# VectorE's instructions kept in source order through the middle of a four-layer transformer kernel, with the split queries' rest written in place

## The chip, the cores and the metric

The kernel runs on one core of one Trainium2 chip. The time is the device time of one execution in microseconds (us); of several executions the median is given. A profiled execution of the same program gives the trace. The engines are TensorE (PE: matrix products and transposes; PEld its weight loads), VectorE (DVE), ScalarE (ACT), GpSimd (POOL) and SyncE (SP, which issues the DMAs here). Each engine runs its own list of instructions, and semaphores make one engine wait for another.

## The reference

Four layers run one after the other over x, four batches of 512 tokens by 512 channels, each added to x with a gate. Cut to what matters:

```python
def _wkv(w, u, k, v):                 # a scan over the tokens, for each channel
    def step(carry, kv_t):
        p, q, o = carry
        no = jnp.maximum(o, u + kt); A = jnp.exp(o - no); E = jnp.exp(u + kt - no)
        y = (A * p + E * vt) / (A * q + E)
        no2 = jnp.maximum(w + o, kt); A2 = jnp.exp(w + o - no2); E2 = jnp.exp(kt - no2)
        return ((A2 * p + E2 * vt, A2 * q + E2, no2), y)

def _L0_ffn_ref(x, w1, w2, w3):       # 512 -> 2048 -> 512
    # _bitlinear(x, w): x in int8 steps by groups of 64, w by its sign and mean magnitude
    h = jax.nn.silu(_bitlinear(x, w1)) * _bitlinear(x, w2)
    return _bitlinear(h, w3)

def _L1_xattn_ref(x, cond, wq, bq, wkv, bkv, wp, bp):    # 16 heads of 32
    q = _qdq(x) @ _qdq(wq).T + bq                        # _qdq: int8 steps, a scale for each row
    k, v = jnp.split(cond @ wkv.T + bkv, 2, axis=-1)
    attn = jax.nn.softmax(jnp.einsum('bnhd,bmhd->bhnm', q, k) * scale, axis=-1)
    o = jnp.einsum('bhnm,bmhd->bnhd', attn, v).reshape(B, N, C)
    return _qdq(o) @ _qdq(wp).T + bp

def _L1_ffn_ref(x, gamma, W):         # rms norm, int8 steps, W in {-1, 0, 1}
    return jnp.einsum('bsd,od->bso', x_ste, w_ste)

x = x + tanh(g_xattn[0]) * _L0_xattn_ref(..., _layernorm(x), ctx)    # WKV
x = x + tanh(g_ffn[0]) * _L0_ffn_ref(_layernorm(x), ...)             # FFN
x = x + tanh(g_xattn[1]) * _L1_xattn_ref(_layernorm(x), ctx, ...)    # attention
x = x + tanh(g_ffn[1]) * _L1_ffn_ref(_layernorm(x), ...)             # ternary
```

## The kernel before, in words

**Merged streams.** Each layer of each batch is a Python generator that emits some instructions and yields. `line(gen, parts)` gives a generator places, a number for each of its steps, on one axis; `run(until)` always advances the generator with the lowest place, and so several layers of different batches are merged into one stream of emitted instructions. The unit of the axis is a batch, cut in `SLOTS` = 17 slots, one for each of the 16 units of an FFN and one more. In the steady part the FFN of batch b runs in the slots from b on, beside the WKV layer of batch b+1 and the attention of batch b−1, which begins some five slots later. The ternary layer of a batch comes after its attention's output projection. `run(0.99)` emits the first part, with the weights' preparation under way, inside a block with its own pools; after it the attention's pool is opened, and `run(NB + 9)` emits all that remains. There are NB = 4 batches; the last attention runs from place 4.29 on.

**The order on the engines.** The order of emission is not the order of execution. A list scheduler sorts the instructions of each engine by its own estimates of when their inputs are ready. TensorE is bound to the source: `matmul()` and `transpose()` go through `in_turn`, and `next_turn()` moves on the instruction behind which those of the next step must stand (L162, L165 are these helpers, so every matmul and transpose has one of these two lines). VectorE, ScalarE, POOL and SP have no such bond. A block `tc.manual_schedule(engines={...})` takes the order of emission for the engines named.

**An FFN unit** is a block of 128 tokens (t) by 512 hidden channels (f). Two products of eight matmuls each go to ff_hp. ScalarE takes the tanh (L745), VectorE makes the gate (L746) and the product with the second half (L750). `quantised` then brings the result to int8 steps: the maximum by groups (L222, tile qg_s), its scale (L676, L678), the product rounded to int8 (L680) on VectorE, a cast on ScalarE (L684), and a product on POOL (L685). `parts` transposes the result (tp_ps), and writes it as a rounded half (ScalarE, L696) and the rest (VectorE, L697). The down product goes to ff_acc, which L773 adds to x.

**The WKV layer** of batches 1 to 3 is four chains of 128 channels, eight steps apart. In each VectorE has the scans L599, L629 and L634, the product L632, the reciprocals L640 (two halves), the product L645 and the addition L653; POOL has L608, L628, L630, L635, L636, L641 and L642.

**The attention.** `prepared` (L219 POOL, then at_s by L222, L226, L227 on VectorE, L231 ScalarE, transposes qr_ps) brings the rows of x to int8 steps. `project(g)` makes the queries of 128 channels: VectorE's L898 into q, ScalarE's L903 with the rounded half, VectorE's L904 with the rest, and two DMAs on SP to qD, from where the units' queries are fetched again (at_qR). Its tiles q and half, as at_xn, tf_xn and at_y, are rows of one pool tag, at_row, with `ROWS` = 3 buffers. A unit is a pair of heads by 256 tokens: scores s_ps, their maximum (VectorE, L948, one number for each row), the exponentials with their sum (ScalarE, L950), transposes pt_ps, copies (ScalarE, L970), the product with the values o_ps (L990 copies it), and `collect` (ot_ps; L998 and L1000 on VectorE). `project_out` makes the scale at_s of the output rows (L222, L226, L227), rounds (L231), and after the product VectorE's L1036 and an addition (L1037).

**The ternary layer** centres and scales a row on POOL (L219, L1147, tile tf_xn), takes its maximum and scale on VectorE (tile tf_s: L222, L1151, L1152, L1158, L1159), rounds on ScalarE (L231), transposes (qr_ps), multiplies (f_ps), adds (L1172) and writes the output.

**PSUM** has eight banks. After the first part, three (hp) are shared by ff_hp and s_ps, three (m) by most transposes and small products, and two are ff_acc.

Of the kernel before, what the change touches and what calls it, by code (L numbers as in the profile page):

```python
# [11 lines left out]
F32R = mybir.dt.float32r  # L12
# [18 lines left out]
def kernel(  # L31
# [37 lines left out]
    NB, T, D = x.shape  # L69
# [61 lines left out]
    def bank(name, dtype=F32):  # L131

        return psum_tile(name, "m", dtype)
# [22 lines left out]
    def next_turn():  # L156

        if "last" in turn:
            turn["ahead"] = turn["last"]

    def matmul(*args, **kwargs):
        return in_turn(nc.tensor.matmul(*args, **kwargs))  # L162
# [677 lines left out]
    def attention_layer(b, xb, pool, tiles=range(NT)):  # L840
# [5 lines left out]
        lo, n = tiles[0] * P, len(tiles) * P  # L846
# [9 lines left out]
        def row(name, dtype=F32):  # L856
            return pool.tile([P, D], dtype, name=name, tag="at_row", bufs=ROWS)
# [29 lines left out]
        def project(g):  # L887
            qp = bank("q_ps")[:, 0:n]
            for c in range(NC):
                matmul(  # L890
                    qp,
                    lhsT=wqT[:, c, g * P : (g + 1) * P],
                    rhs=xqT[:, c, lo : lo + n],
                    start=(c == 0),
                    stop=(c == NC - 1),
                )
            q = row("at_q")[:, 0:n]
            nc.vector.scalar_tensor_tensor(  # L898
                q, qp, sq[:, g : g + 1], sxb[:, lo : lo + n], ALU.mult, ALU.mult
            )  # L900
            half = [row("at_half", F32R)[:, 0:n] for _ in range(2)]
            bias = bqc[:, g : g + 1]
            nc.scalar.activation(half[0], q, AF.Identity, bias=bias)  # L903
            nc.vector.scalar_tensor_tensor(  # L904
                half[1], q, bias, half[0].bitcast(F32), ALU.add, ALU.subtract
            )
            for i in range(2):
                nc.sync.dma_start(out=qD[b][g][i, :, lo : lo + n], in_=half[i].bitcast(F32))
# [83 lines left out]
        def collect(k):  # L992
# [14 lines left out]
            )  # L1007

        project(0)
        fetch_keys(0)  # L1010
        fetch_values(0)
        fetch_queries(0)
        yield
        project(1)
        fetch_queries(1)
        yield
# [45 lines left out]
        for k in range(len(units) + 2):  # L1062
# [29 lines left out]
            if now:  # L1092
                p, h = units[k]
                if h == 0:
                    if p + 1 < NP:
                        fetch_keys(p + 1)
                    if p % 2 == 0 and p // 2 + 2 < NC:
                        next_turn()
                        project(p // 2 + 2)
                elif p % 2 and p // 2 + 1 < NC:  # L1100
                    fetch_values(p // 2 + 1)
                if k + 2 < len(units):
                    fetch_queries(k + 2)
# [72 lines left out]
    def ternary_layer(b, xb, pool):  # L1176
        if b == NB - 2:
            r, scale = statistics(b, xb, range(NT))
            yield
        else:  # L1180
            r, scale = layernorm(xb, rms=True, pinned=False), None
        yield from in_steps([ternary(b, xb, pool, t, r, scale) for t in range(NT)], 1)
# [9 lines left out]
    def late(make):  # L1192
        yield from make()

    def place(line):

        k = line["step"]
        for start, end, steps in line["parts"]:
            if k < steps:
                at = start + (end - start) * k / steps  # L1200

                return (math.floor(at * SLOTS) + 0.8) / SLOTS if line["aside"] else at
            k -= steps
        return end

    def run(until):
        while lines:
            now = min(lines, key=place)
            if place(now) > until:
                return  # L1210
            try:
                next(now["gen"])
                now["step"] += 1
                next_turn()
            except StopIteration:
                lines.remove(now)
# [5 lines left out]
    def line(gen, *parts, aside=False):  # L1222
        lines.append({"gen": gen, "parts": parts, "step": 0, "aside": aside})
# [124 lines left out]
    for b in range(NB):  # L1348
        if b:
            early = (0.99, 1.0, 4) if b == 1 else (b - 0.19, b - 0.1, 3), (b - 0.08, b, 1)  # L1350
            line(
                late(lambda b=b: ffn_layer(xs[b])),
                *((early[0],) if b == 1 else early),
                (b, b + 16 / SLOTS, 64),
                (b + 16 / SLOTS, b + 17.75 / SLOTS, 7),
            )
        start = b + 1 + 4.95 / SLOTS
        end = start + 18 / SLOTS
        line(
            late(lambda b=b: attention_layer(b, xs[b], at)),  # L1360
            (b + 1.0 if b == 0 else b + 0.7, b + 1.03 if b == 0 else b + 0.9, 5),
            (b + 1 + 1.7 / SLOTS, b + 1 + 3.7 / SLOTS, 5),
            (b + 1 + 3.75 / SLOTS, b + 1 + 4.35 / SLOTS, 2),
            (start, end, 72),
            (end, end + 2.4 / SLOTS, 6)
            if b != NB - 2
            else (end - 0.15 / SLOTS, end + 4.65 / SLOTS, 6),
            (end + 2.4 / SLOTS, end + 3.4 / SLOTS, 4),
        )
        if b < NB - 1:  # L1370
            line(
                late(lambda b=b: ternary_layer(b, xs[b], at)),
                (end + 3 / SLOTS, end + 8 / SLOTS, 8)
                if b < NB - 2
                else (end + 4.85 / SLOTS, end + 11.85 / SLOTS, 7),
                aside=b < NB - 2,
            )
    run(NB + 9)


# [43 lines left out]
```

## Time and profile before

| | |
|---|---|
| median of 3 runs | 1096.12 us (1095.92 to 1096.5) |
| the profiled execution | 1094.21 us |
| its span, first to last instruction | 1092.4 us |
| its mean granted TensorE clock | 0.956 |
| PE busy | 943.3 us (86% of the span) |
| VectorE busy | 827.0 us (76%), 1600 instructions |
| ScalarE busy | 729.9 us (67%) |
| POOL busy | 320.7 us (29%) |
| DMA | 189.68 MB, mean 174 GB/s |
| 0 to 316 us (first part) | PE busy 262.98, VectorE 214.17 |
| 316 to 330 us | PE busy 9.42, VectorE 11.57 |
| 330 to 1092.4 us | PE busy 670.87, VectorE 601.26 |

A line of a timeline or a group reads: start and duration in us (or busy time and mean), engine, source line, operation, the tile written and after the arrow the tiles read, shape and type, and "xN" where N like instructions are drawn together. A bracket at its end gives the idle time of that engine just before and, after the arrow, the instruction on another engine that ended it.

The page also draws the span in 40 equal slices of 27.3 us; a digit is the busy share in tenths:

```profile
PE   3879997998879888799997886999999999878975
DVE  5985548757876899896769898966687866579976
PEclk8889999999999999999999798999999999989998
```

After the first part PE's row dips twice, in the 14th to 17th slice (355 to 464 us: 8 8 8 7) and in the 22nd to 25th (573 to 683 us: 7 8 8 6); VectorE's row is at 8 to 9 there.

### The profile page before, as it was taken

To read this page: it belongs to the slowest core of one execution; us is meant where nothing else is said; L and a number is where in the kernel's file an instruction comes from. 1 tells how busy PE (TensorE), PEld (TensorE's weight loads), DVE (VectorE), ACT (ScalarE), POOL (GpSimd) and SP (SyncE) were. 2 spreads that over 40 slices of the span, in tenths; PEclk is the share of its full clock that TensorE was granted. 3 is DMA by queue.
4 is the path that set the end of the run, shared out by engine and by line. 5 is a ranking of instruction groups with operands and counts; after the bars stand their busy time and mean duration, and the time that the engine had idled before them with its cause. 6 is when DMAs were issued, how large, how long until landed. Compare 5 with 4: busy or idle time off the path is not lost.

```text
span 1092.4 us, 17928 instructions
## 1 busy us (share of the span) xinstructions
PE 943.3 (86%) x6350; PEld 680.0 (62%) x6380; DVE 827.0 (76%) x1600; ACT 729.9 (67%) x1490; POOL 320.7 (29%) x328
## 2 busy tenths in 40 slices
PE   3879997998879888799997886999999999878975
PEld 2345564565557666677775665677776777655652
DVE  5985548757876899896769898966687866579976
ACT  5656755567545776667877576677685777877863
POOL 3831104423333254621215545412122410100000
PEclk8889999999999999999999798999999999989998
DMA  8188845464445674645576354655574563244311
GB/s 288 39 272 317 323 169 190 144 221 155 154 146 181 221 234 127 231 129 169 185 234 204 121 177 133 204 195 180 184 231 156 184 210 116 59 148 116 116 42 39
DMA packets 85674, 189.68 MB, mean 174 GB/s; under 512 B 12241, under 2 KB 36817, under 8 KB 74577
## 3 DMA queue, kind: packets, MB, share of 16 engines
q1 hardware_dynamic: 85584, 188.53, 51.7%
q8 instruction: 51, 0.84, 0.3%
q14 instruction: 39, 0.31, 0.1%
HBM read 148.65 MB, written 39.85 MB: 173 GB/s over the span
## 4 chain that ended last, share of the span: by engine, by line
PE 49%; DVE 22%; ACT 14%; POOL 5%; issue 5%; DMA 4%; SPq 1%; ACTq 0%; POOLq 0%; DVEq 0%
PE ff_hp L162 15%; PE pt_ps L165 7%; PE ff_acc L162 6%; PE o_ps L162 4%; PE v_ps L162 4%; PE s_ps L162 3%; ACT at_P L950 3%; DVE wk_q L640 3%; ACT at_PT L970 3%; DVE at_nm L948 2%; PE k_ps L162 2%; DVE wk_p L634 1%; PE qr_ps L165 1%; PE tp_ps L165 1%; ACT wk_e L612 1%
## 5 line engine op out<-in xcount | busy, mean ns | idle before, releaser
L162 PE MATMUL ff_hp<-wT,xp 128*128 128x512 f32 x1024 | 275.7, 412 | 6.6 <-DVE ff_z L746 3.7
L162 PEld LDWEIGHTS ff_hp<-wT,xp 128*128 128x128 f32 x1024 | 195.4, 196 | 54.6 <-DVE ff_z L746 5.7
L950 ACT ACTIVATE at_P<-s_ps,at_nm 128x512 f32<-128x512 f32 x256 | 175.0, 690 | 45.2 <-DVE at_nm L948 43.4
L948 DVE TENSOR_REDUCE at_nm<-s_ps 128x1 f32<-128x512 f32 x256 | 166.6, 677 | 38.4 <-PE s_ps L162 37.9
L970 ACT COPY at_PT<-pt_ps 128x512 f32<-128x512 f32 x224 | 131.2, 590 | 72.6 <-PE pt_ps L165 71.9
L685 POOL TENSOR_TENSOR ff_z<-qg_b,qg_s 128x512 f32<-128x512 bf16 x64 | 71.9, 1124 | 314.6 <-ACT qg_b L684 304.7
L165 PE MATMUL pt_ps<-ident,at_P 128*128 128x128 f32 x1024 | 155.4, 280 | 9.0 <-ACT at_PT L970 4.3
L165 PEld LDWEIGHTS pt_ps<-ident,at_P 128*128 128x128 f32 x1024 | 118.1, 142 | 47.3 <-ACT at_PT L970 10.9
L162 PE MATMUL ff_acc<-wT,hr 128*128 128x512 f32 x512 | 137.6, 409 | 5.2 <-DVE hr L697 2.6
L162 PE MATMUL s_ps<-at_kR,at_qR 128*128 128x512 f32 x256 | 103.0, 464 | 24.0 <-ACT at_P L950 17.6
L162 PEld LDWEIGHTS ff_acc<-wT,hr 128*128 128x128 f32 x512 | 92.9, 191 | 26.2 <-DVE hr L697 4.2
L162 PE MATMUL o_ps<-at_PT,at_V 128*32 128x128 f32 x2048 | 75.4, 281 | 4.7 <-ACT at_PT L970 2.8
L162 PEld LDWEIGHTS o_ps<-at_PT,at_V 128*32 128x32 f32 x2048 | 54.8, 111 | 28.6 <-issue 11.6
L746 DVE SCALAR_TENSOR_TENSOR ff_z<-ff_z,ff_hp 128x512 f32<-128x512 f32 x64 | 43.4, 679 | 37.0 <-ACT ff_z L745 36.9
L745 ACT ACTIVATE ff_z<-ff_hp,coef 128x512 f32<-128x512 f32 x64 | 44.1, 688 | 40.5 <-PE ff_hp L162 38.1
L750 DVE SCALAR_TENSOR_TENSOR ff_z<-ff_hp,coef,ff_z 128x512 f32<-128x512 f32 x64 | 47.7, 745 | 30.2 <-PE ff_hp L162 30.1
L684 ACT CAST qg_b<-qg_i 128x512 bf16<-128x512 int8 x80 | 49.3, 617 | 27.4 <-DVE qg_i L680 17.3
L162 PEld LDWEIGHTS s_ps<-at_kR,at_qR 128*128 128x128 f32 x256 | 43.3, 194 | 36.4 <-ACT at_P L950 25.2
L162 PE MATMUL v_ps<-wkvT,cT 128*128 128x512 f32 x128 | 60.5, 618 | 5.5 <-DVE wT L303 2.3
L162 PE MATMUL k_ps<-cT,wkvT 128*128 128x512 f32 x128 | 61.3, 631 | 2.3 <-ACT wk_k L584 1.0
L640 DVE RECIPROCAL wk_q<-wk_q 128x256 f32<-128x256 f32 x32 | 54.5, 1722 | 3.0 <-POOL wk_q L635 1.6
L696 ACT CAST hr<-tp_ps 128x512 fp32r<-128x512 f32 x64 | 37.6, 588 | 21.7 <-PE tp_ps L165 21.7
(180 smaller groups left out, 1669.4 us busy)
## 6 DMA issues: line engine op xcount, KB each, us to landing
wT<-wD SPq DMA_DIRECT2D x72, 1024.0 KB, 5.4
wn<-in_L_ffn_w_dram SPq DMA_DIRECT2D x18, 1024.0 KB, 6.2
at_kR<-kD SPq DMA_DIRECT2D x128, 128.0 KB, 4.0
at_qR<-qD SPq DMA_DIRECT2D x256, 64.0 KB, 2.5
wD<-wT SPq DMA_DIRECT2D x12, 1024.0 KB, 4.2
kD<-k_half SPq DMA_DIRECT2D x16, 512.0 KB, 2.8
qD<-at_half SPq DMA_DIRECT2D x32, 256.0 KB, 2.2
cn<-in_ctx_dram SPq DMA_DIRECT2D x8, 512.0 KB, 5.9
```

What stands on the lines that cost most here:

```text
L162: return in_turn(nc.tensor.matmul(*args, **kwargs))
L165: return in_turn(nc.tensor.transpose(*args))
L640: nc.vector.reciprocal(half, half)
L684: nc.scalar.copy(qb, qi)
L685: nc.gpsimd.tensor_tensor(grouped(src), grouped(qb), s.unsqueeze(2).to_broadcast([P, NG, GS]), ALU.mult)
L696: nc.scalar.copy(part[:, 0, :], pt)
L745: nc.scalar.activation(z, hp, AF.Tanh, scale=coef[:, 0:1])
L746: nc.vector.scalar_tensor_tensor(z, z, 1.0, hp, ALU.add, ALU.mult)
L750: nc.vector.scalar_tensor_tensor(z, hp, coef[:, 1:2], z, ALU.mult, ALU.mult)
L948: nc.vector.tensor_reduce(nm, sp, AX.X, ALU.max, negate=True)
L950: nc.scalar.activation(lanes[k, i, t], sp, AF.Exp, bias=nm, accum_out=sums[k][:, t, i : i + 1],)
L970: made[k] = nc.scalar.copy(dst, blocks(pt))
```

## The change

Two edits. In `project` the rest of the queries is no longer a row of its own: it is written over q, which is its input. And between the end of the first part and place NB + 0.4 = 4.4, everything is emitted inside a block in which VectorE takes the order of emission; from 4.4 on, the order is the scheduler's again, as it is before place 0.99.

```diff
-            half = [row("at_half", F32R)[:, 0:n] for _ in range(2)]
+            half = [row("at_half", F32R)[:, 0:n], q.bitcast(F32R)]
             bias = bqc[:, g : g + 1]
             nc.scalar.activation(half[0], q, AF.Identity, bias=bias)
             nc.vector.scalar_tensor_tensor(
@@
+    with tc.manual_schedule(engines={mybir.EngineType.DVE}):
+        run(NB + 0.4)
     run(NB + 9)
```

## The prediction

> **What bounds the kernel now.** I read three views: the table by stage, the timeline of TensorE at its longest stall, and VectorE's timeline around that stall and in a quiet unit.
>
> The table by stage cuts the profiled execution where the work beside the FFN changes: microseconds, then the busy time of each engine with its instructions, then TensorE's granted clock.
>
> ```profile
> 370.00:470.00 100.00, 84.43 (x574) 64.86 (x575) 94.57 (x148) 69.48 (x145) 50.76 (x50) 0.95 0.57 186
> 470.00:570.00 100.00, 96.01 (x786) 75.74 (x788) 73.82 (x172) 76.03 (x168) 20.76 (x22) 1.00 0.56 185
> 570.00:692.00 122.00, 96.88 (x643) 73.11 (x641) 108.78 (x193) 81.88 (x163) 64.61 (x62) 0.90 0.52 168
> 692.00:790.00 98.00, 95.14 (x760) 74.37 (x761) 69.36 (x159) 71.35 (x158) 20.80 (x21) 1.00 0.58 193
> ```
>
> Columns two and four are TensorE and VectorE. From 470 to 570 and from 692 to 790 TensorE is busy 96 and 97% and sets the pace. In the two stretches that carry the WKV of batch 2 (370 to 470, "stretch 1") and batch 3 (570 to 692, "stretch 2"), TensorE falls to 84 and 79%, and VectorE is the fullest engine: 95 and 89%. VectorE idles 5.4 us in stretch 1 and 13.2 us in stretch 2. Only in these two, and in the 14 us between the first part and 330, can VectorE's order gain time; in the rest it can only lose some.
>
> Why stretch 2 idles more shows on TensorE's timeline (start, duration, last in brackets the idle time before and what ended it):
>
> ```profile
> 651.85 0.60 PE L165 MATMUL tp_ps<-ident,ff_z 128*128 128x128 f32 x4
> 661.05 1.11 PE L165 MATMUL qr_ps<-ident,tf_xn 128*128 128x128 f32 x4 [8.60 <-ACT tf_xn L231]
> ```
>
> The ternary layer's transposes wait 8.6 us for a row that ScalarE rounds at 660.18, and ScalarE waits for a scale from VectorE. That scale is five small operations, and VectorE's timeline shows where they stand:
>
> ```profile
> 639.79 0.69 DVE L222 TENSOR_REDUCE tf_s<-tf_xn 128x1 f32<-128x512 f32 x1 [0.40 <-POOL tf_xn L1147]
> ...
> 657.07 0.10 DVE L1151 TENSOR_SCALAR tf_s<-tf_s 128x1 f32<-128x1 f32 x1
> ...
> 658.80 0.15 DVE L1152 RECIPROCAL tf_s<-tf_s 128x1 f32<-128x1 f32 x1
> 658.88 1.15 DVE L1159 TENSOR_TENSOR tf_s<-tf_s,coef 128x1 f32<-128x1 f32 x1
> ...
> 660.03 0.12 DVE L1158 TENSOR_SCALAR tf_s<-tf_s 128x1 f32<-128x1 f32 x1
> ```
>
> Between the maximum at 639.79 and the next link lie 17 us of other work that the scheduler put first. The output projection's scale is torn in the same way (L222 594.70, L226 596.13, L227 597.92) and TensorE stands 3.87 us before 599.47; 2.70 us more stand ahead of 615.65, where transposes wait for L1036. Together 15.2 us of TensorE stall in stretch 2, and after each the matmuls are slow for a while: eight ff_hp at 663.67 take 3.32 us, against 2.01 elsewhere.
>
> **The change, part by part.** It adds and removes no instruction. VectorE takes its work in the order in which the code emits it from the end of the first part (about 316 us) to place 4.4, the first two units of the last attention (about 950 us). The other engines keep the scheduler's orders; those move in places, as the built kernels show: POOL's L608 and L598 now stand behind L685, and single pt_ps transposes change sides with s_ps.
>
> In an FFN unit the source emits L222, L676, L678, L680 as one run; the scheduler interleaves other work. A run of dependent links is slower:
>
> ```profile
> 336.56 0.69 DVE L222 TENSOR_REDUCE qg_s<-ff_z 128x8 f32<-128x512 f32 x1
> 337.28 0.17 DVE L676 TENSOR_SCALAR qg_s<-qg_s 128x8 f32<-128x8 f32 x1
> 337.48 0.20 DVE L678 RECIPROCAL qg_r<-qg_s 128x8 f32<-128x8 f32 x1
> 337.72 0.69 DVE L680 TENSOR_TENSOR qg_i<-ff_z,qg_r 128x512 int8<-128x512 f32 x1
> ```
>
> From start to start, medians over the trace: L750 to L222 785 ns (668 with something else next), L222 to L676 702 (600), L676 to L678 205 (70), L678 to L680 237 (118). That is 1.93 against 1.45 us: 0.48 lost for each unit. Stretch 1 and 2 hold some 8 units each, so +3.8 us each.
>
> The projections of the queries (L898, ScalarE's L903, L904) become adjacent on VectorE: L904 waits there for ScalarE, with everything behind it. Three adjacent pairs in this trace run 1.59, 1.59 and 1.95 us from start to start, against 0.67 when not held, so the wait is 0.9 to 1.3; I take 1.1. Two projections for each stretch: +2.2 each. Behind L904 stands L697 of the same unit, which the down projection wants. The Trainium skill, page "PSUM — Partial Sum Buffer", section "Engine vs sequencer instructions", calls VectorE's queue strictly first in, first out; the interleaved case avoids that hold, so the rule speaks against the change, and priced by the three rows it is this same +2.2.
>
> The in-place edit is free in instructions. It takes two rows of the three-buffer pool for a projection instead of three. In this trace L904 of the projection at 641.8 stood until 662.3, after the stalled transposes of tf_xn had given their row back. In strict source order L904 stands ahead of the very chain that would free that row, so I read the edit as what makes the order possible, and cost it at 0. Its cover: the second write to qD must read q before that row is reused, and a qD write lands 2.2 us after issue, while the next projection comes a unit (10 us) later. Without this cover it costs 2.2 us each.
>
> Two-input operations on VectorE take longer beside POOL. L632 lasts 1.33 us on average; where it follows L629 directly, it takes 0.69 and POOL's L630 the delay (1.72 against 1.28):
>
> ```profile
> 610.23 0.69 DVE L632 TENSOR_TENSOR wk_q<-wk_e,wk_q 128x512 f32<-128x512 f32 x1
> ```
>
> The source always has L629, L632 adjacent, so L632's excess leaves: 2.6 us in stretch 1 and 1.6 in stretch 2. The Trainium skill, "SBUF — State Buffer", section "Who interferes with whom", makes this an exclusive lock on a shared port pair; by it the loser waits out the whole other operation (1.28 us for L630), where the rows show about 0.7 lost, and the sum by it would be some 2 us a stretch better. L904's excess (1.0 beside L630 in stretch 1) leaves too, as L904 stands elsewhere, and the excess of L1159 and L198 (2.9 in stretch 2), since the tf_s chain closes up. I can't exclude that other pairs collide anew: the excess over all lines is 7.1 and 9.1 us, so the bounds of this term are −3.6 to +3.6 in stretch 1, −4.5 to +4.5 in stretch 2.
>
> The torn chains close. In source order the at_s and tf_s chains are consecutive (about 2 us from L222 to the last link instead of 20 and 4), so the stalls of 8.6 and 3.9 us should go, and VectorE's idle time in stretch 2 should fall to stretch 1's: 13.2 − 5.4 = −7.8. Bounds: 0 (VectorE is refilled by other waits) and −13.2 (all idle time gone). In stretch 1 VectorE waited 1.9 us for at_xn from POOL; the source places that row two steps ahead: −1.9.
>
> What is late next in source order is L948, the maximum of the next scores: it stands behind the whole run, and the three banks shared by s_ps and ff_hp are held until then. In the forecast TensorE has enough slack here (16 to 21% idle) to hide it; its price is in the rivals.
>
> Sums. Stretch 1: −2.6 −1.0 +3.8 +2.2 −1.9 = +0.5. Stretch 2: −7.8 −1.6 −2.9 +3.8 +2.2 = −6.3. From 316 to 330 TensorE stalls 4.3 us, of which 1.30 is for a scale of at_s (L226 at 326.79): −1.3 (bounds −4.3 and +2, the latter two L904 waits). The other stages are TensorE's, whose order hardly moves: 0. Total −7.1, from 1094.2 (the profiled execution; its span is 1092.4) to 1087.1. The median of the runs is 1.9 above the profiled execution: 1089.
>
> **Rivals.**
>
> *A larger gain.* All three TensorE stalls of stretch 2 (15.2 us) go, and the slow matmuls after them: 1096.1 − 15.2 = 1080.9, about 1080 with a tenth of slow matmuls. For it: TensorE's granted clock is 0.90 there, against 1.00 beside it. Against: VectorE has 108.8 us of work there, and 122 − 108.8 = 13.2 is all it can give.
>
> *Refilled.* The idle time of stretch 2 only changes its reason (ScalarE's tanh for L746, the scores for L948): −7.8 becomes about −2, the sum −1.3, and the time 1094.8 to 1095: no change that a measurement of this kernel can tell (0.2%, or 2.2 us). For it: VectorE still idled 5 us in the 16 us after the 8.6 us stall.
>
> *Late maxima: slower.* In the source's order of a unit with WKV work, the first L948 comes 0.79 + 0.70 + 0.21 + 0.24 + 0.60 (L680) + 0.36 (L998, L1000) + 0.60 (L697) + about 1.8 (L629, L632) = 5.3 us after L750; the scheduler put it there 2.2 and 2.8 us after (425.78 to 427.95, 414.97 to 417.80). So s_ps banks come free 2.5 us later. The trace has five such stalls of TensorE already in stretch 1 (0.9 to 2.2, mean 1.5). If this decides in all eight units with WKV work, it is 8 × 1.5 = +12: 1089 + 12 = 1101. It decides once the lateness exceeds TensorE's slack of some 2 us a unit (16 of 100 us over 8 units). Against: PE's own order places the scores after a block of ff_hp (2 us) and ahead of transposes that need no new bank.
>
> That the order doesn't take hold is no rival: the built kernel shows VectorE's instructions in source order throughout.
>
> **Numbers.** Forecast 0.46, larger gain 0.10, refilled 0.14, late maxima 0.30. Thus faster by over 0.2% is 0.56, within it 0.14, slower 0.30. The forecast's own range is 1084 to 1094 (the port term and the idle bound of stretch 2, −5 to +5). The range to hold the time 8 times in 10 takes in most of both neighbours: 1080 to 1103.
>
> **What would show it.** Right: the wait of qr_ps for tf_xn is under 2 us; stretch 2 is 5 to 8 us shorter and stretch 1 within 2 us; L632 has a mean near 0.7; L904 waits for ScalarE about 1 us in each projection; TensorE's clock in stretch 2 rises above 0.90. Wrong: s_ps or ff_hp waiting for at_P L950 or L746 more than the 6.5 us of stretch 1; VectorE's idle time in stretch 2 staying at 13; or a time lost from 692 to 900, where I put nothing.

## The result and the profile after

The changed kernel takes 1190.08 us (median of 4 runs, 1189.09 to 1190.85), the kernel before 1096.02 (4 runs). The ratio is 1.0864, 95% interval [1.0851, 1.0877]: some 94 us slower, where the forecast was 1089 and the range ended at 1103.

The rows of the page of the changed kernel that answer to those shown of before (40 slices, now of 29.7 us):

```profile
PE   4879988889868788859987858779889789878885
DVE  5976457577666788855768887656777676659977
PEclk8879999989998899979998989889999899979998
```

After its second slice VectorE's row has no 9 before the 37th, where before it had six from the 15th to the 26th, and TensorE's 9s stand alone or in pairs. No engine is full for long. Two tables by stage show where this begins. They are cut at the same FFN units in both kernels (VectorE's L750 of the first FFN's unit 15, of units 5 and 13 of the second and third, and of units 5 and 15 of the last): the stretch, its length, then the busy time of TensorE, its weight loads, VectorE, ScalarE and POOL, TensorE's granted clock, the DMA's share and GB/s. First the kernel before:

```profile
313.40:373.90 60.50, 53.23 (x250) 40.28 (x249) 44.61 (x92) 31.48 (x56) 21.01 (x23) 0.94 0.63 200
373.90:478.30 104.40, 89.04 (x627) 69.37 (x629) 98.34 (x161) 73.41 (x157) 50.42 (x49) 0.95 0.57 183
478.30:576.10 97.80, 93.75 (x752) 73.57 (x752) 70.83 (x162) 74.88 (x164) 21.61 (x23) 1.00 0.57 190
576.10:703.20 127.10, 102.03 (x686) 77.33 (x690) 114.05 (x212) 85.29 (x172) 66.23 (x62) 0.91 0.50 165
703.20:797.40 94.20, 91.34 (x732) 71.31 (x734) 65.17 (x146) 69.67 (x156) 18.33 (x19) 1.00 0.58 191
797.40:917.20 119.80, 115.16 (x850) 89.52 (x855) 87.65 (x198) 82.79 (x183) 31.36 (x31) 0.99 0.57 186
917.20:1092.40 175.20, 138.34 (x1371) 96.80 (x1380) 134.76 (x312) 122.99 (x296) 9.21 (x10) 0.95 0.29 86
```

And the changed kernel:

```profile
313.90:385.60 71.70, 53.62 (x244) 40.09 (x243) 45.75 (x93) 31.12 (x54) 20.65 (x22) 0.93 0.54 168
385.60:501.60 116.00, 93.94 (x634) 71.43 (x635) 96.01 (x152) 75.31 (x157) 50.10 (x51) 0.94 0.52 171
501.60:620.10 118.50, 98.69 (x746) 76.41 (x746) 77.12 (x163) 75.57 (x163) 20.27 (x23) 0.93 0.48 155
620.10:763.50 143.40, 104.63 (x691) 78.96 (x696) 113.71 (x203) 86.15 (x172) 64.94 (x61) 0.89 0.45 143
763.50:873.00 109.50, 95.74 (x733) 73.40 (x734) 72.65 (x153) 70.08 (x156) 17.65 (x19) 0.97 0.52 167
873.00:1006.50 133.50, 116.74 (x850) 90.04 (x856) 93.50 (x203) 86.95 (x185) 31.48 (x31) 0.97 0.51 165
1006.50:1187.30 180.80, 140.03 (x1371) 99.41 (x1380) 136.92 (x314) 123.99 (x295) 9.22 (x10) 0.93 0.29 83
```

The stretches grew by 11.2, 11.6, 20.7, 16.3, 15.3, 13.7 and 5.6 us; the first part, ahead of the change, by 0.5. So the loss is nowhere in particular. It is also in the stretches that TensorE filled to 96%, which the prediction put down as 0. VectorE's own busy time rose by 20.3 us in these seven rows, and the time in which it stood idle (length less busy) by 74: it has little more to do and waits far more. TensorE shows the same: 20.5 us more busy, at a lower clock, and 74 more idle.

The view of waits says whom the engines stood for over the whole span (total in us, times, longest). First the kernel before, where L904 still wrote at_half, then the changed kernel:

```profile
PE s_ps L162 <- ACT at_P L950: 17.6, 19, 2.2
DVE at_half L904 <- ACT at_half L903: 4.3, 6, 1.2
DVE hr L697 <- ACT hr L696: 10.3, 9, 4.6
DVE qg_s L222 <- ACT ff_xn L215: 3.4, 3, 1.4
PE qr_ps L165 <- ACT tf_xn L231: 16.2, 4, 8.6
```

```profile
PE s_ps L162 <- ACT at_P L950: 51.4, 31, 8.7
DVE at_q L904 <- ACT at_half L903: 26.4, 15, 4.0
DVE hr L697 <- ACT hr L696: 21.7, 13, 4.6
DVE qg_s L222 <- ACT ff_xn L215: 21.8, 5, 8.8
PE qr_ps L165 <- ACT tf_xn L231: 32.5, 8, 10.7
```

VectorE's three are of one kind: ScalarE must answer, and the source has the use of the answer next in VectorE's line. Of the wait at L697, 8.9 us lie in the first part in both kernels, ahead of the change: behind it the wait went from 1.3 to 12.8 us.

The torn chain that the prediction was built on is closed now, and the stall behind it is longer. VectorE and then TensorE around it (start, duration, idle time before in brackets):

```profile
701.20 3.37 DVE L640 RECIPROCAL wk_q<-wk_q 128x256 f32<-128x256 f32 x2 [1.11 <-POOL wk_q L635]
704.48 1.22 DVE L948 TENSOR_REDUCE at_nm<-s_ps 128x1 f32<-128x512 f32 x2
705.61 0.74 DVE L750 SCALAR_TENSOR_TENSOR ff_z<-ff_hp,coef,ff_z 128x512 f32<-128x512 f32 x1
...
710.87 0.68 DVE L222 TENSOR_REDUCE tf_s<-tf_xn 128x1 f32<-128x512 f32 x1
...
712.04 0.15 DVE L1159 TENSOR_TENSOR tf_s<-tf_s,coef 128x1 f32<-128x1 f32 x1
```

```profile
713.02 1.11 PE L165 MATMUL qr_ps<-ident,tf_xn 128*128 128x128 f32 x4 [10.70 <-ACT tf_xn L231]
```

L222 to L1159 now take 1.3 us instead of 20. But the whole chain stands where the source has it, behind the unit's reciprocals, maxima and quantisation, and VectorE worked without a pause from 701.2 to 712. TensorE waits 10.70 us instead of 8.60.

The second longest stall, 8.73 us for the scores at 519.92, lies in the entry of the third FFN, where VectorE makes two layer norms (L191 and what follows) while the second FFN still runs. The maxima that TensorE needed stand behind them:

```profile
511.02 0.69 DVE L222 TENSOR_REDUCE qg_s<-ff_xn 128x8 f32<-128x512 f32 x1 [2.20 <-ACT ff_xn L215]
...
517.24 1.27 DVE L948 TENSOR_REDUCE at_nm<-s_ps 128x1 f32<-128x512 f32 x2
```

Between these two lines VectorE has no pause either. So in both of TensorE's longest stalls VectorE was at work most of the time, on something that the source has first.

### The profile page after: what moved, and what is told of

It reads as the page before. It is cut to its first block, busy times and chain, and to the rows that moved or that the text cites. A ratio compares the mean times of both kernels' runs of the same rounds, so it can differ in the third digit from the quotient of the medians.

```text
span 1187.3 us, 18031 instructions
## 1 busy us (share of the span) xinstructions
PE 963.2 (81%) x6350; PEld 691.4 (58%) x6380; DVE 847.1 (71%) x1600; ACT 739.0 (62%) x1490; POOL 316.9 (27%) x328
## 4 chain that ended last, share of the span: by engine, by line
PE 45%; DVE 27%; ACT 17%; issue 5%; DMA 3%; POOL 3%; SPq 1%; DVEq 0%; ACTq 0%; POOLq 0%
PE ff_hp L162 14%; PE pt_ps L165 6%; PE ff_acc L162 6%; PE o_ps L162 4%; PE s_ps L162 4%; ACT at_P L950 3%; DVE at_nm L948 3%; DVE wk_q L640 2%; ACT at_PT L970 2%; PE v_ps L162 2%; ACT wk_e L612 2%; PE k_ps L162 2%; DVE qg_s L222 2%; DVE qg_i L680 2%; PE qr_ps L165 2%
## 5 line engine op out<-in xcount | busy, mean ns | idle before, releaser
L162 PE MATMUL ff_hp<-wT,xp 128*128 128x512 f32 x1024 | 283.1, 420 | 3.8 <-ACT at_P L950 1.8
L162 PEld LDWEIGHTS ff_hp<-wT,xp 128*128 128x128 f32 x1024 | 201.3, 202 | 53.9 <-ACT at_P L950 5.1
L950 ACT ACTIVATE at_P<-s_ps,at_nm 128x512 f32<-128x512 f32 x256 | 174.0, 687 | 37.9 <-DVE at_nm L948 37.6
L970 ACT COPY at_PT<-pt_ps 128x512 f32<-128x512 f32 x224 | 131.3, 590 | 89.8 <-PE pt_ps L165 88.8
L685 POOL TENSOR_TENSOR ff_z<-qg_b,qg_s 128x512 f32<-128x512 bf16 x64 | 68.2, 1066 | 393.5 <-ACT qg_b L684 388.9
L165 PE MATMUL pt_ps<-ident,at_P 128*128 128x128 f32 x1024 | 158.7, 285 | 8.5 <-ACT at_PT L970 2.5
L162 PE MATMUL s_ps<-at_kR,at_qR 128*128 128x512 f32 x256 | 107.5, 484 | 54.9 <-ACT at_P L950 51.4
L165 PEld LDWEIGHTS pt_ps<-ident,at_P 128*128 128x128 f32 x1024 | 121.6, 145 | 46.5 <-issue 10.4
L162 PEld LDWEIGHTS s_ps<-at_kR,at_qR 128*128 128x128 f32 x256 | 45.7, 203 | 70.0 <-ACT at_P L950 61.3
L750 DVE SCALAR_TENSOR_TENSOR ff_z<-ff_hp,coef,ff_z 128x512 f32<-128x512 f32 x64 | 47.8, 747 | 43.0 <-PE ff_hp L162 43.0
L697 DVE TENSOR_TENSOR hr<-tp_ps,hr 128x512 fp32r<-128x512 f32 x64 | 43.7, 684 | 21.8 <-ACT hr L696 21.7
```

Source lines behind the costliest of these rows:

```text
L165: return in_turn(nc.tensor.transpose(*args))
L685: nc.gpsimd.tensor_tensor(grouped(src), grouped(qb), s.unsqueeze(2).to_broadcast([P, NG, GS]), ALU.mult)
L697: nc.vector.tensor_tensor(part[:, 1, :], pt, part[:, 0, :].bitcast(F32), ALU.subtract)
L750: nc.vector.scalar_tensor_tensor(z, hp, coef[:, 1:2], z, ALU.mult, ALU.mult)
L950: nc.scalar.activation(lanes[k, i, t], sp, AF.Exp, bias=nm, accum_out=sums[k][:, t, i : i + 1],)
L970: made[k] = nc.scalar.copy(dst, blocks(pt))
```

## The experiments

Each run's ratio is to the kernel before on the same chip. H, C, M, I, L, R and S are the theories as the expectations name them. In what follows "the second FFN's WKV stretch" is the second row of the tables, stretches of experiments are cut at the same units, and idle time is a stretch's length less the engine's busy time in it.

**In place alone.** The kernel before with the first edit only.

> Before, with the rest of the queries written over q and nothing else. Theory H (held queue: VectorE in strict order stands at round trips through ScalarE and POOL, with all later work behind it), theory C (crossed orders: ScalarE's and POOL's lists, made by the scheduler, don't fit VectorE's) and theory M (late maxima: L948 behind the run of the quantisation) all put the loss on the order, so 1096 us within 3. Theory I (the rest written in place makes L904, L903 or the writes to qD wait): well above, up to 1190.

Measured: 1097.80 us, 1.0029 [1.0018, 1.0040]. Theory I falls: the 94 us are the order's. But the edit isn't free either. It adds some 3 us, since the scheduler, given another use of the rows, orders a few places otherwise. How the strict order does without the in-place edit was not run.

**The order over less.**

```diff
     with tc.manual_schedule(engines={mybir.EngineType.DVE}):
-        run(NB + 0.4)
+        run(1.85)
```

> VectorE's strict order ends at place 1.85 instead of 4.4 (the scheduler has the rest). H, C and M: the loss is made all along and not given back by the later stages, which TensorE fills, so what the changed kernel had lost by unit 14 of the second FFN, 23 to 40 us, stays: 1119 to 1136 us. If the loss sits in one place behind 1.85, or later slack takes it up: 1096 to 1105.

Measured: 1135.23 us, 1.0376 [1.0347, 1.0404]. From the third FFN on, a unit takes what it took in the kernel before, to within 0.1 us in most, and the 41 us lost by then are 40 at the end of the last FFN. The loss is local, and nothing behind it gives it back.

**ScalarE too.**

```diff
-    with tc.manual_schedule(engines={mybir.EngineType.DVE}):
-        run(NB + 0.4)
+    with tc.manual_schedule(engines={mybir.EngineType.DVE, mybir.EngineType.Activation}):
+        run(1.85)
```

> As the run before, to place 1.85, but ScalarE takes the source's order too. C: the two lists agree, and most of the loss goes: 1096 to 1108 us. H: the round trips stay, since VectorE still waits at L904, L697 and L222 for ScalarE: within 10 us of the run before or slower than it.

Measured: 1158.74 us, 1.0582 [1.0564, 1.0601]. Another 23.5 us on top, so C falls: here two lists in one order are worse than one.

**The FFN's entry.** In unit 14 of the second and of the third FFN, where the next FFN's rows are made ready, the changed kernel takes 29.3 and 24.7 us, before 12.7 and 12.7. The first try moved the layer norm half a slot ahead.

```diff
         r = layernorm(xb)
+        if apart:
+            yield
...
-            early = (0.99, 1.0, 4) if b == 1 else (b - 0.19, b - 0.1, 3), (b - 0.08, b, 1)
+            early = (0.99, 1.0, 4) if b == 1 else (b - 0.22, b - 0.22, 1), (b - 0.19, b - 0.1, 3), (b - 0.08, b, 1)
```

> The changed kernel, with the FFN's layer norm of batches 2 and 3 emitted half a slot ahead of the rows that need it. H: VectorE no longer stands at L222 of ff_xn (11.0 and 9.3 us in the trace; the time around these two places grew by 16.5 and 12 us), so 20 to 28 us come back: 1162 to 1170 us. C and M: under 5 us, 1185 to 1190.

Measured: 1182.75 us, 1.0807 [1.0791, 1.0823]: 7.3 us back, where H expected 20 to 28. The trace of this run shows why (ScalarE, then VectorE):

```profile
527.51 0.81 ACT L215 ACTIVATE ff_xn<-xb,ln_r 128x512 f32<-128x512 f32 x1 [0.32 <-PE tp_ps L165]
```

```profile
528.35 0.69 DVE L222 TENSOR_REDUCE qg_s<-ff_xn 128x8 f32<-128x512 f32 x1 [10.37 <-ACT ff_xn L215]
```

VectorE stands 10.4 us for a row that ScalarE can't write until TensorE has read an older row of the same three buffers. TensorE came to that read (tp_ps) at 526.84 only, after a wait of 2.75 us for at_P and eight slow ff_hp (3.35 us). The maxima for that at_P had been done at 516.12, ahead of this L222. So the second row was moved behind that step as well:

```diff
-            early = (0.99, 1.0, 4) if b == 1 else (b - 0.19, b - 0.1, 3), (b - 0.08, b, 1)
+            early = (0.99, 1.0, 4) if b == 1 else (b - 0.22, b - 0.22, 1), (b - 0.19, b - 0.19, 1), (b - 1 + 14.8 / SLOTS, b - 1 + 14.96 / SLOTS, 2), (b - 0.08, b, 1)
```

> The run with the layer norm apart gave back 4.3 us by its trace, and VectorE still stood 10.4 us at L222 of the second ff_xn row: ScalarE's L215 waited there for a buffer (tag ff_a, three of them) that TensorE frees a step later, in work that itself waited for VectorE's next maxima. Here the second row and its quantisation are emitted after that step as well. H: the waits at L222 of ff_xn fall below 2 us in all, and the units around both entries, which took 29.3 and 24.7 us against 12.7 in the kernel before, come to 14 to 17: 1160 to 1170 us. If the buffer wasn't it: 1180 to 1185.

Measured: 1176.63 us, 1.0754 [1.0735, 1.0773]: 13.5 us back (12 by the two ratios), and 6.6 us above H's range. The units at the entries take 19.6 and 14.8 us, and the wait at L222 is gone:

```profile
528.62 0.68 DVE L222 TENSOR_REDUCE qg_s<-ff_xn 128x8 f32<-128x512 f32 x1
```

That is 19.6 us less in the two, of which a third was lost again elsewhere. This is the only place where an edit to the order gave back a known part of the loss.

**The other answers, one at a time.** L904 with its DMAs, L697, and the quantisation were each emitted a step later, behind the next unit's two maxima.

```diff
-            nc.vector.scalar_tensor_tensor(
-                half[1], q, bias, half[0].bitcast(F32), ALU.add, ALU.subtract
-            )
+            def rest():
+                nc.vector.scalar_tensor_tensor(
+                    half[1], q, bias, half[0].bitcast(F32), ALU.add, ALU.subtract
+                )
...
             for i in range(2):
                 if now:
                     scores(k, i, 0)
+            if owed:
+                owed.pop()()
```

> The changed kernel, with L904 and its two DMAs emitted a step after L903, behind the next two maxima. H: VectorE's wait at L904, 26.4 us in 15 places in the changed kernel's trace, falls below 5, and 10 to 25 us come back: 1165 to 1180. M: the maxima are late for the quantisation's sake, so under 5 us: 1185 to 1192.

Measured: 1188.43 us, 1.0861 [1.0839, 1.0882]: no gain. The wait at L904 fell to 1.0 us, and the one at L697 rose from 21.7 to 30.9.

```diff
+            while owed_hr:
+                owed_hr.pop(0)()
             if now:
                 t, f = units[n]
```

> The changed kernel, with L697 of hr emitted a step after ScalarE's L696, behind the next two maxima. H: VectorE's wait at L697 (some 13 us in the ordered stretch) goes, the maxima come 0.6 us to 3 us earlier, and the units with WKV work fall from 17.4 towards 16: 10 to 25 us, 1165 to 1180. M in its narrow form (only the quantisation's run counts): under 8 us.

Measured: 1207.22 us, 1.1036 [1.1018, 1.1055], 17 us slower. Now TensorE waits for L697 itself (this run's view of waits, then that of the run with all four edits further down; their L699 is L697):

```profile
PE ff_acc L162 <- DVE hr L699: 52.0, 21, 9.4
```

```profile
PE ff_acc L162 <- DVE hr L699: 79.2, 29, 7.8
```

The same row of the changed kernel has 7.5 us. TensorE's wait for the scores did fall, from 51.4 to 23.4: what was freed on one side was paid on the other.

```diff
-            hidden[t, f] = quantised(z)
+            owed_q.append((t, f, z))
...
+            while owed_q:
+                *at_q, z = owed_q.pop()
+                hidden[tuple(at_q)] = quantised(z)
             if now:
                 t, f = units[n]
```

> The changed kernel, with the whole quantisation of a unit (L222, L676, L678, L680, L684, L685) emitted behind the next unit's first two maxima. The first of them then comes about 1.9 us earlier in each of 48 units. M: PE's wait of s_ps for at_P, 51.4 us, falls to 20 or less, and 30 to 70 us come back: 1120 to 1160. H: the wait at L904 and L697 stays, and holds the maxima as before: 1175 to 1195.

Measured: 1191.94 us, 1.0893 [1.0871, 1.0914], and 50.8 us of waiting for the scores. M falls in this form: with the run out of the maxima's way, neither the wait for the scores nor the time changes for the better.

**All of them at once** (the entry, L904, L697 and the quantisation).

> The entry moved, and L904, L697 and the quantisation each emitted behind the next two maxima, all in one kernel. H: the waits add up when they are all taken away, though each alone came back at the next hand-over: 1120 to 1155 us. Theory L (lockstep: a fixed list can't fill any wait with other work, so VectorE's idle time of 19 us in the second FFN's WKV stretch, units 5 to 13, only changes its reason): 17 to 30 us of idle time there, and 1165 to 1195 us.

Measured: 1196.48 us, 1.0936 [1.0912, 1.0960]. The waits don't add up as H has it. TensorE's wait for the scores did fall, to 15.3 us, but its wait for L697 rose to 79.2. VectorE's idle time in the second FFN's WKV stretch, 6.1 us before and 20.0 after, was 19.3, 20.1, 29.8 and 24.4 in the last four runs: it changed its reason and did not shrink. The time is 1.5 us over L's bound, and H's is 41 away.

**ScalarE's answers first.** A higher priority for L696, L903 and L950 in the changed kernel, and its control in the kernel before.

```diff
+        with tc.high_priority():
             nc.scalar.copy(part[:, 0, :], pt)
```

> The changed kernel with a higher priority in the scheduler for ScalarE's answers L696, L903 and L950, so that they stand ahead of the WKV exponentials (L612, L614) and of L684 in ScalarE's list. C in a second form (the order is good, and only ScalarE's list makes the answers late): VectorE's waits at L697 and L904 fall below 10 of 48 us, and 20 to 50 us come back, 1140 to 1170. L: what is put behind comes late in its place, 1180 to 1200.

> The control of the run before: the same priority in the kernel before, where VectorE's order is the scheduler's. C second form and L: little to gain where VectorE can do other work meanwhile, 1090 to 1105.

Measured: 1191.14 us, 1.0876 [1.0860, 1.0892], and 1100.21 us, 1.0045 [1.0029, 1.0062]. VectorE's wait at L697 fell from 21.7 to 11.1 us, but the one at L904 stayed, 25.2 after 26.4: of the 48 us only 12 went, where C wanted them below 10. So C in its second form has no support, but this run can't exclude it. The control shows something else: in it the fourth row's stretch takes 122.6 us instead of 127.1, with 8.3 us of idle time on VectorE instead of 13.1, and the second row's takes 111.5 instead of 104.4. So some of the idle time that the prediction counted on can go, but here more time was lost elsewhere.

**The scale chains alone.** The kernel before with a higher priority for the at_s and tf_s chains and L231: what the prediction hoped for, without the strict order.

```diff
+            with tc.high_priority():
                 absmax(s[:, 0:1], xn)
                 int8_scale(s[:, 0:1], s[:, 1:2], s[:, 0:1])
                 rounded(xn, s[:, 1:2])
```

> The kernel before, with a higher priority for the scale chains alone (at_s: L222, L226, L227; tf_s: L222, L1151, L1152, L1158, L1159; and ScalarE's L231), and nothing else of the change. If the torn chain cost what the prediction put on it (TensorE's stalls of 8.6 and 3.9 us, VectorE's idle time −7.8): 1086 to 1090. If VectorE's work in that stretch is what sets the pace and the stall only shows where it is paid: 1093 to 1098.

Measured: 1110.00 us, 1.0133 [1.0117, 1.0149], slower. The stretch with the two stalls (fourth row of the tables) took 125.2 us against 127.1. There the stalls of 8.60 and 3.87 us are gone, and TensorE waits in other places of the same stretch (the run's timeline, TensorE; its L971 is L970):

```profile
642.74 0.63 PE L165 MATMUL tp_ps<-ident,ff_z 128*128 128x128 f32 x4 [3.22 <-DVE qg_s L676]
...
657.05 0.66 PE L165 MATMUL qr_ps<-ident,tf_xn 128*128 128x128 f32 x4 [3.31 <-ACT at_PT L971]
...
673.90 1.08 PE L165 MATMUL tp_ps<-ident,ff_z 128*128 128x128 f32 x4 [3.90 <-ACT at_PT L971]
```

VectorE's idle time in this stretch went from 13.1 us to 11.8. So the stall was where the pace of VectorE's work came to light rather than its cause: closing the chain this way is worth 1.9 us there, not 7.8. The rest of the 15 us was lost elsewhere, 11 of them in the last two rows' stretches.

**Which orders cost.** VectorE's instructions bound one behind the other by hand in the source's order, with one class left to the scheduler.

```diff
+    def in_order(ins):
+        if "on" in held:
+            if "last" in held:
+                behind(ins, held["last"])
+            held["last"] = ins
+        return ins
...
-    with tc.manual_schedule(engines={mybir.EngineType.DVE}):
-        run(NB + 0.4)
+    held["on"] = True
+    run(NB + 0.4)
+    held.clear()
```

> VectorE's instructions in the changed kernel's order, bound one behind the other, but for the maxima L948, which the scheduler may place. L (nothing may pass a wait, so any class that may pass gives back part): TensorE's wait of s_ps for at_P falls from 51 to about 20 us, 1140 to 1170. M (the late maxima are the cause): 1095 to 1115. R (the dependent runs' own slowness, 0.48 us in each of 48 units, and what follows): 1180 to 1192.

> As the run before, but the WKV's work (L599, L629, L632, L634, L640, L645, L653) is free and the maxima are bound. L: it fills the waits in the two stretches that carry it, which lost 11.6 and 16.4 us, and nothing elsewhere: 1160 to 1178. M: under 10 us, 1182 to 1192. If WKV's place in the list is the cause: below 1130.

> The maxima and the WKV's work free, all else bound. L: the two gains add up, and the entries of the FFN (28 us in the changed kernel) and its first units (11 us) stay lost: 1115 to 1150. M: as with the maxima alone, within 5 us.

Measured: 1205.72 us, 1.1013 [1.0996, 1.1030]; 1195.27 us, 1.0921 [1.0906, 1.0936]; 1207.85 us, 1.1036 [1.1022, 1.1050]. All three are slower than the changed kernel, so L's forecast of the time failed, though with the maxima free TensorE's wait for the scores fell nearly as far as it had said, from 51.4 to 24.9 us (13.4 with both free). So M as the cause falls too, and work that may pass does not by itself fill the waits. With the WKV's work free, the second FFN's WKV stretch did come down from 116.0 to 112.3 us, but the third FFN's went up from 143.4 to 151.5. What is free is set among bound work by the scheduler's estimates; that these were worse here than the source's order is the likely reason, not a shown one. A run with all of VectorE's work bound by hand was not made.

> With the rest of the queries in place, and of VectorE's work only the FFN's (L676, L678, L680, L697, L746, L750, L773) bound in the source's order among themselves; maxima, WKV, attention, norms and ternary are the scheduler's. Order between streams (a theory S): within one stream the scheduler's order is nearly the source's, so 1096 to 1108. R or H (the run of the quantisation, L697 waiting for ScalarE): a large part of the 94 us, 1130 to 1190.

> The reverse: the FFN's seven lines are the scheduler's, and all other work of VectorE is bound in the source's order. S: attention, WKV, norms and ternary still stand in a fixed order between them, and most of the loss stays: 1140 to 1190. R or H: 1096 to 1130.

Measured: 1113.35 us, 1.0157 [1.0127, 1.0187], and 1162.42 us, 1.0622 [1.0590, 1.0654]. Binding the FFN's seven lines among themselves costs 18.7 us (3 of them the in-place edit's), 5 more than S allowed; binding everything but them costs 67.7 (the same 3 among them). With the in-place edit counted once, the two make 83 of the 94. The second list also holds the FFN's own maxima L222, which the seven lines leave out; in it unit 14 of the second and of the third FFN takes 22.8 and 18.9 us, together 16 more than in the kernel before. So the larger part comes with attention, WKV, norms, ternary and L222 in a fixed order. How much of it lies between these streams, how much inside one, and which pair carries what stays open. R falls by the second run: there the quantisation's four instructions stand in a row in 1 unit of 49 (in the changed kernel in 48), and most of the loss is there all the same.

**A version that might beat both.** ScalarE's priority had shortened two units of the third FFN in the kernel before and lengthened others; here it holds from place 2.46 to 2.75 alone.

> The kernel before, with the priority of ScalarE's L696, L903 and L950 from place 2.46 to 2.75 alone. Where that priority held everywhere, units 8 and 11 of the third FFN (where TensorE's stall of 8.6 us lies) took 13.8 and 12.2 us instead of 18.6 and 19.4, and unit 7 took 25.3 instead of 18.8. If the gain can be had without that loss: 1083 to 1090. If the stretch is paced by VectorE's work and units only trade time among them: 1092 to 1098.

Measured: 1092.66 us over 12 runs, 0.9985 [0.9973, 0.9997]. The gain, if it is one, is 1.4 us; its stretch is 2.1 shorter. Units traded time with each other, as the second reading had it.

## Why the prediction was wrong

The reading of the bound fits the table: in two stretches VectorE is the fullest engine, in the rest TensorE. Two of the signs that the prediction had named for being wrong came, TensorE's wait for at_P and the time lost from 692 to 900. Of the steps:

- *The torn chains close, −7.8.* Wrong in kind, and the step that set the sign. The stall was read as the fault of the chain's order. With the chain closed alone the stretch gained 1.9 us, with the strict order it lost 16.3, and VectorE's idle time in it, which was to fall by 7.8 us, rose from 13.1 to 29.7. In a stretch where VectorE is 89% busy, TensorE waits for VectorE's work in one place or another: with the two stalls of 8.60 and 3.87 us gone, others of 3.22, 3.31 and 3.90 us stood in the same stretch.
- *The other stages, 0.* The largest error: rows one, three, five, six and seven of the tables lost 66.5 us of the 94 (for the first 14 us of row one the sum had −1.3, read off a wait at 326.79 that stands before TensorE's transposes of ff_xn). The step priced a stage by who fills it on average. But VectorE, in strict order, can stop TensorE in a stage in which it is 72% busy, when what TensorE needs stands behind other work, or behind an instruction that waits. The worst is the FFN's entry (16.6 and 12.0 us over the kernel before), and no term of the sum named the layer norms and the L222 that stand there ahead of the next maxima.
- *L904, 1.1 us each.* Right mechanism, low price: 26.4 us in 15 places, 1.76 each. The same kind of wait at L697 rose from 10.3 to 21.7 us and was named only as standing behind L904.
- *The quantisation's run, 0.48 us a unit, and L632.* Both seen. VectorE's busy time rose by 20.3 us in the seven rows; 48 units at 0.48 would make 23, less 4 for L632, whose mean fell from 1013 to 757 ns. That this comes near is partly luck: added up from the trace, the run accounts for some 16 us, and other instructions that now stand right behind what they depend on, such as L1000 (4.3), for much of the rest. And the sum counted 16 units only:

```profile
L904 DVE SCALAR_TENSOR_TENSOR at_q<-at_q,bqc,at_half 128x512 fp32r<-128x512 f32 x16 | 12.2, 762 | 26.4 <-ACT at_half L903 26.4
L632 DVE TENSOR_TENSOR wk_q<-wk_e,wk_q 128x512 f32<-128x512 f32 x16 | 12.1, 757 | 0.9
```

- *The in-place edit, 0.* It measures +0.29% alone.
- *The rival of the late maxima* had the side and the place: TensorE's wait of s_ps for at_P tripled, from 17.6 to 51.4 us. Its price, eight units at 1.5 us, was too small, and its cause too narrow: the longest of these stalls, 8.73 us, is outside the units with WKV work and behind a layer norm. With the quantisation emitted behind the maxima the wait stayed, and where the maxima were left to the scheduler it halved and the time didn't come back.

So what is shown: the strict order makes the loss, at once where it holds and for good; either of the two groups that were bound alone costs; 12 to 13.5 us come back at the FFN's entry; the waits at L904 and L697, taken away one at a time or together, gave nothing back, as others grew. What is not shown is a count of the rest by pairs of streams. Nor is VectorE's list alone in having changed: the scheduler made ScalarE's and POOL's lists anew around it, and some 220 of ScalarE's 1490 instructions and 50 of POOL's 328 stand elsewhere among the others. No run kept those lists and changed VectorE's alone, so their part is open. The argument that it is lockstep, each engine's list fixed against the others so that what is late stops all that is behind it, fits the four runs in which the uses of the answers were emitted later, but it remains an argument, and the three runs with a class left to the scheduler show that letting one class pass doesn't cure it.

## What to carry to other kernels

Before an engine is put in source order, list each of its instructions that waits for another engine's answer, here L904, L697 and the entry's L222, and walk each round trip with the queues and buffers on the way, in the stages where that engine isn't full as well. Look too for long work of its own, here the layer norms, that the source has ahead of something another engine needs at once. A stall of one engine in a stretch that another engine fills is a symptom: price its removal by the full engine's idle time that can really go, and try it alone first. Where the order of many streams was made by a scheduler, binding a part of it can be worse than binding all.

## What the hardware showed besides

20 of the 94 us are not TensorE's waits: it is busy that much longer with the same matmuls. In the changed kernel, just behind its stall at the FFN's entry:

```profile
519.92 1.22 PE L162 MATMUL s_ps<-at_kR,at_qR 128*128 128x512 f32 x2 [8.73 <-ACT at_P L950]
520.94 3.62 PE L162 MATMUL ff_hp<-wT,xp 128*128 128x512 f32 x8
```

The eight ff_hp at the same place took 2.01 us at 488.97 in the kernel before, where nothing had stalled. TensorE's granted clock was 0.50 from 519.92 to 525.20 in the changed kernel, and 1.00 from 488.42 to 491.00 in the kernel before. Over the third row of the tables it fell from 1.00 to 0.93, and TensorE's busy time rose by 4.9 us with 6 matmul records fewer. Over all seven rows the clock stood at 0.5 for some 61 us before and 109 after, and TensorE was busy in 50 and 80 us of these; at half the speed, the 30 us more are worth some 15 us (an estimate), the larger part of the 20.

The Trainium skill, page "TensorE: Matmul & The Clock Gate", section "What's actually happening", says that the clock falls to half after an idle window of about 3.4 us, until a window of work has passed. The stall of 8.73 us agrees with that: in its trace the clock is at 0.5 from 515.8, 4.6 us after TensorE's last work, to 526.0, 6.1 us after its work began again. The prediction named the slow matmuls only as something that the change might end; a change that makes long stalls pays for them a second time in the matmuls behind them.
